# Two layers of a perceiver: VectorE's side work of a turn split in two parts, one ahead of each copy of transposed exponentials

## The chip, the cores and the metric

The kernel runs on one core of one Trainium2 chip. The metric is device time in microseconds (us) of one execution; the times given are medians of several runs. TensorE is called PE here, VectorE DVE, ScalarE ACT, GpSimd POOL and SyncE SP, as in the profile.

## The reference

The input x holds 64 sequences of 32 rows with 256 features, the context 64 sequences of 257 rows. Six blocks are added to x one after the other; each works on a layer norm of x:

```python
x = x + L0_xattn(layernorm(x), ctx, ctx)   # 16 heads of 16, rope, a window of 65 keys
x = x + L0_attn(layernorm(x))              # causal self-attention, rope
x = x + L0_ffn(layernorm(x))               # linear with fp8 rounding, below
x = x + L1_xattn(layernorm(x), ctx, ctx)   # softmax attention over all 257 keys
x = x + L1_mixer(layernorm(x))             # gated cumulative sum plus a convolution, below
x = x + L1_moe(layernorm(x))               # shared expert + top 2 of 8 experts, exact gelu

# L0_ffn, per row
scale = max(amax(abs(x)), 1e-12) / 448
A = (x / scale).astype(float8_e4m3fn).astype(f32) * scale
out = A @ (weight * weight_scale).T + bias

# L1_mixer
h = relu(x @ gate_w1 + gate_b1); gate = sigmoid(h @ gate_w2 + gate_b2)
glob = gate * (x @ U_w) * cumsum(x @ V_w, axis=1)
t_out = x[s-1] * conv_w[:, 0] + x[s] * conv_w[:, 1] + x[s+1] * conv_w[:, 2]
out = t_out + glob @ out_w + out_b
```

## The kernel before, in words

The 2048 rows of x lie in SBUF as 4 groups (g) of 4 tiles (t) of 128 rows, so 16 tiles; a tile is 4 sequences.

**Layer 0.** `small_attentions` (line 247) runs both small attentions as one pipeline of tiles; an iteration of its loop `for t` takes one tile through each of several stages. Behind the transposes of an iteration it calls a generator of side work twice (lines 588 and 589). For the last iterations that generator is `first_sides` (line 1431), which steps the fp8 linear of group 0.

**The fp8 linear** is the generator `linear(g)` (line 683), for one group of 512 rows: the norm; the row maxima `am` and from them the scales `xsc`, `rsc`, `osc` (three small VectorE instructions); the scaling of y by rsc (four GpSimd instructions); then, for each pair of tiles, `rounded(pair)` (line 709): two instructions that make `big` out of the exponent bits of y, and two sums that round, y + big and from that q = y - big. `by_feature` (line 723) transposes both q on PE (into ps_qT, copied by ScalarE), and `outputs` multiplies (ps_ff) and adds to x, scaled by osc. Each `yield` ends a step.

**Layer 1's cross-attention** (`cross_attention`, line 1018) is where most of the time lies: 16 tiles of 4 turns (b, one sequence each), 64 turns, numbered 0 to 63 here, and a tail. A turn mixes stages of two or three tiles. In its order in the loop (lines 1374 to 1405):

1. `turned(before, b, 0, eT)`: 4 PE transposes of the exponentials e of the tile before into ps_t, and a VectorE copy of that to eT.
2. `weights()`: the softmax sums of the turn before: VectorE's reciprocal, which waits for ScalarE's last exponential, then GpSimd's scaling of e (four instructions) by it.
3. `own_heads()` (every second turn): two VectorE instructions that take ps_o into own; the first waits for lv from GpSimd. In turn b = 1 `project` (ps_p, added to x by VectorE).
4. `values` (ps_v, 8 matmuls), copied by ScalarE.
5. `turned(before, b, 1, eT)`: the other 4 transposes. ps_t has a single bank, so they wait for the copy of step 1. Copied by VectorE, in the last tile by ScalarE.
6. `next(side, None)`: one step of side work.
7. `keys` of the next tile (ps_k), `scores` of this tile (ps_s, 16 matmuls into 4 banks; for each bank a VectorE reduction, which subtracts the mask and finds the row's extreme, and ScalarE's exponential), in turn b = 1 `last_keys` (ps_le, lv), `context` (ps_o, which reads eT and v).

All instructions of these stages keep their written order on each engine: a VectorE instruction that waits holds back everything written after it. So the order in the program is the order in each queue.

**The side work** of turn 16g and after is `side_work(g + 1)` (line 1326): linear(g + 1), then norm and queries of the next group. The row maxima with the scales come in turns 3, 19 and 35; `rounded(0)` in turns 5, 21, 37; `rounded(1)` in turns 6, 22, 38; `by_feature` of both pairs in turns 7, 23, 39. In the last 16 turns it is `late_pieces` (line 989): the mixers of groups 0, 1, 2 and the first half of 3, and the layer norms of the last block, each started at its own turn.

**The mixer** (`mixer`, line 764): norm; yT = transposed y (psT); ps_huv, scanned by VectorE; the gate (ps_g); for each of two channels c a matmul (ps_d) and three VectorE passes that make the convolution `conv` (taps 1, 0, 2; 128x512 elements, the first reads ps_d); then conv is transposed back (ps_x) and added to x. psT, ps_huv, ps_g, ps_d, ps_x, ps_qT, ps_ff, ps_k and ps_v share a ring of PSUM banks, so each also waits until an earlier tenant of its bank has been read. Channel 0's passes of mixers 0, 1, 2 lie in turns 55, 58, 61, channel 1's in 56, 59, 62, and ps_x in 57, 60, 63.

**The mixture** (`mixture`, line 1475) follows: router, top 2, experts. It also steps the mixer of the last two tiles (`last_mixer`).

Most instructions pass through one helper, so their line in the profile is 107 (all but PE), 119 (matmuls) or 122 (PE transposes); the names of the tiles tell them apart.

Of the kernel before, what the change touches and what calls it, by code (L numbers as in the profile page):

```python
# [11 lines left out]
AF = mybir.ActivationFunctionType  # L12
ALU = mybir.AluOpType
# [5 lines left out]
NB, S, SK = 64, 32, 257  # L19
H, DH = 16, 16  # L20
NG, NT = 4, 4
# [44 lines left out]
def perceiver_kernel(ctx: ExitStack, tc: tile.TileContext, a: dict, out: bass.AP):  # L66
# [613 lines left out]
        )  # L680
        yield

    def linear(g):

        x = xs[g]
        y = yield from norm_steps(g)

        for t in range(NT // 2):
            gpsimd.tensor_tensor(x[:, t], x[:, t], row(R_FF), ALU.add)
        yield  # L690
        am = small.tile([P, NT], F32, tag="am", name="am")
        vector.tensor_reduce(am, y, AX.X, ALU.max, apply_absolute_value=True)
        xsc = small.tile([P, NT], F32, tag="xsc", name="xsc")
        vector.tensor_scalar(xsc, am, 1e-12, 1.0 / 448.0, ALU.max, ALU.mult)
        rsc = small.tile([P, NT], F32, tag="rsc", name="rsc")
        vector.reciprocal(rsc, xsc)
        osc = small.tile([P, NT], F32, tag="osc", name="osc")
        vector.tensor_scalar(osc, xsc, vec[:, V_WS : V_WS + 1], None, ALU.mult)
        for t in range(NT // 2, NT):
            gpsimd.tensor_tensor(x[:, t], x[:, t], row(R_FF), ALU.add)  # L700
        yield
        for t in range(NT):
            gpsimd.tensor_scalar(
                y[:, t], y[:, t], rsc[:, t : t + 1], 1.0, ALU.mult, ALU.mult
            )
        yield
        qs, qTs = [], []

        def rounded(pair):


            v = y[:, 2 * pair : 2 * pair + 2, :]
            big = sb.tile([P, 2, D], F32, tag="big", name="big")
            vector.tensor_scalar(
                big.bitcast(I32), v.bitcast(I32), 0x7F800000, None, ALU.bitwise_and
            )
            vector.tensor_scalar(big, big, 2.0**-6, 1.5 * 2.0**20, ALU.max, ALU.mult)
            vector.tensor_tensor(v, v, big, ALU.add)
            q = sb.tile([P, 2, D], BF16, tag=f"fq{pair}", name="q")
            vector.tensor_tensor(q, v, big, ALU.subtract)  # L720
            qs.append(q)

        def by_feature(pair):
            ps = shared_bank[0]([P, 2, 2 * P], "ps_qT", BF16)
            for c in range(2):
                for i in range(2):
                    turn(ps[:, c, i * P : (i + 1) * P], qs[pair][:, i, c * P : (c + 1) * P], ident_bf)
            qT = sb.tile([P, 2, 2 * P], BF16, tag=f"fqT{pair}", name="qT8")
            scalar.copy(qT, ps)
            qTs.append(qT)  # L730

        def outputs(pair):
            ps = shared_bank[0]([P, 2, D], "ps_ff")
            for i in range(2):
                proj(
                    ps[:, i, :],
                    lambda k: qTs[pair][:, k, i * P : (i + 1) * P],
                    lambda k: w8[:, k, :],
                )
            for i in range(2):  # L740
                t = 2 * pair + i
                x = xs[g][:, t, :]
                vector.scalar_tensor_tensor(
                    x, ps[:, i, :], osc[:, t : t + 1], x, ALU.mult, ALU.add
                )

        rounded(0)
        yield
        rounded(1)
        yield  # L750
        by_feature(0)
        by_feature(1)
        yield
        outputs(0)
        yield
        outputs(1)
# [7 lines left out]
    def mixer(g, ts, eng=None, by_act=True):  # L764

        n, t0, N = len(ts), ts[0], len(ts) * P
        x = xs[g]
        steps = norm_steps(g, eng, True, ts, by_act)
        next(steps)
        yield  # L770
        next(steps)
        yield
        if n > 2:
            next(steps)
            yield
        y = finish(steps)

        for t in ts:
            gpsimd.tensor_tensor(x[:, t], x[:, t], row(R_GO), ALU.add)
        yield  # L780
        yT = transposed(y, shared_bank[0], mixer_yT([P, 2, N], "yT"))
        yield

        ps = shared_bank[0]([P, N], "ps_huv")
        proj(ps, lambda k: narrow[:, k, 0:P], lambda k: yT[:, k, :])
        hub = hubs([P, N], "hub")
        scalar.activation(hub[0:64], ps[0:64], AF.Relu, bias=vec[0:64, V_GB1 : V_GB1 + 1])
        sums = sb.tile([P, N], F32, tag="r2", name="sums")
        for i in range(n):
            at = slice(i * P, (i + 1) * P)  # L790
            vector.tensor_tensor_scan(
                sums[32:64, at], keep[96:P], ps[96:P, at], 0.0, ALU.mult, ALU.add
            )
        vector.scalar_tensor_tensor(hub[64:96], sums[32:64], 0.5, ps[64:96], ALU.mult, ALU.mult)
        yield

        ps = shared_bank[0]([P, N], "ps_g")
        mm(ps, lhsT=gw2, rhs=hub[0:64], start=True, stop=True)
        gate = sums[64:96]
        scalar.activation(gate, ps[64:96], AF.Tanh, bias=half_b[64:96], scale=0.5)  # L800
        vector.scalar_tensor_tensor(hub[64:96], gate, 1.0, hub[64:96], ALU.add, ALU.mult)
        yield
        conv = []
        for c in range(2):
            ps = shared_bank[0]([P, N], "ps_d")
            mm(ps, lhsT=gow[:, c * P : (c + 1) * P], rhs=hub[0:96], start=True, stop=True)

            def tap(i):
                return vec[:, V_CONV + 3 * c + i : V_CONV + 3 * c + i + 1]

            got = convs([P, N], "conv")
            src = yT[:, c, :].rearrange("p (b s) -> p b s", s=S)
            dst = got.rearrange("p (b s) -> p b s", s=S)
            vector.scalar_tensor_tensor(got, yT[:, c, :], tap(1), ps, ALU.mult, ALU.add)
            vector.scalar_tensor_tensor(
                dst[:, :, 1:S], src[:, :, 0 : S - 1], tap(0), dst[:, :, 1:S], ALU.mult, ALU.add
            )
            vector.scalar_tensor_tensor(
                dst[:, :, 0 : S - 1], src[:, :, 1:S], tap(2), dst[:, :, 0 : S - 1], ALU.mult, ALU.add
            )  # L820
            conv.append(got)
            if n > 2 or c == 1:
                yield
        for pair in range(n // 2):
            ps = shared_bank[0]([P, 2, D], "ps_x")
            for i in range(2):
                at = slice((2 * pair + i) * P, (2 * pair + i + 1) * P)
                for c in range(2):
                    turn(ps[:, i, c * P : (c + 1) * P], conv[c][:, at], ident)
            mine = x[:, t0 + 2 * pair : t0 + 2 * pair + 2, :]  # L830
            vector.tensor_tensor(mine, ps, mine, ALU.add)
# [157 lines left out]
    def late_pieces():  # L989
# [12 lines left out]
            (16, last_pieces[1]),  # L1002
        ]
        for now in range(20):
            for first, piece in pieces:
                if now >= first and (now, first) != (19, 14):
                    next(piece, None)
                    if now == first == 13:
                        next(piece)
                    if (now, first) == (18, 13):  # L1010
                        fill_hidden(1)
            fill_hidden({17: 1, 18: 2}.get(now, 0))
            yield
# [4 lines left out]
    def cross_attention(loaded):  # L1018
# [292 lines left out]
        now = fetched.pop(0)  # L1311
# [14 lines left out]
        def side_work(g):  # L1326
# [17 lines left out]
            yield  # L1344
            queries(yT, 1, qT_next[0])

        qT_next = [qT]
        last_sides = late_pieces()


        done, before = None, None
        weights, own_heads = None, None
        for i in range(nt + 2):
            g, t = divmod(i, NT)
            after = None
            if i < nt:
                if t == 0:
                    side = side_work(g + 1) if g + 1 < NG else last_sides
                now.update(g=g, t=t, e=[], qb=qb_next)
                now["last"] = last_([P, 4, 4], "last")  # L1360
                if i + 2 < nt:
# [12 lines left out]
            for b in range(4 if i <= nt else 0):  # L1374
# [7 lines left out]
                weights, own_heads = None, None  # L1382
                if done is not None and b == 1:
                    project(done)
                if before is not None:
                    v = values(before, b)
                    turned(before, b, 1, eT, i == nt - 1)
                    if b == 0:
                        spread(before)
# [40 lines left out]

    def first_sides():

        steps = linear(0)
        yield next(steps)
        yield
        yield next(steps)
        yield next(steps)
        yield next(steps)
        yield next(steps)
        yield  # L1440
        yield next(steps)
        yield
        yield next(steps)
        yield
        yield next(steps)
        yield next(steps)
        finish(steps)
# [27 lines left out]
    def mixture():  # L1475
# [25 lines left out]
        sync.dma_start(out=rc, in_=a["route"])  # L1501
        before_bf = sb.tile([P, 2, P], BF16, tag="fq0", name="before_bf")
        norm_1, norm_2, first_norm = last_pieces
        last_mixer = mixer(3, range(2, 4), vector, False)
        last_norm = normed(3, range(2, 4), vector, False)
        early, late = choose(0, nt - 4), choose(nt - 4, 4)
        warm = small.tile([P, 1], F32, tag="warm", name="warm")
# [537 lines left out]
```

## Time and profile before

| | us |
|---|---|
| median of 3 runs | 910.21 (908.77 to 911.31) |
| the profiled execution | 908.4 |
| its span, first to last instruction | 906.6 |
| PE busy in the span | 852.0 |
| DVE busy | 586.5 |
| POOL busy | 505.4 |
| ACT busy | 428.2 |
| mean granted PE clock | 0.983 |

By stretch, PE is busy for 255.9 of the first 280 us, 49.8 of the next 50, 128.7 of 130 (330 to 460), 127.5 of 130 (460 to 590), 83.0 of 90 (590 to 680), 52.8 of 60 (680 to 740) and 154.4 of the last 166.

A line of a timeline reads: start in us from the span's start, duration, engine, program line, operation, output tile <- input tiles, shapes and types, how many instructions are drawn together; in brackets the engine's idle time just before and the engine and tile whose semaphore ended it. The releaser is inferred; where the engine named had long been done, it was another.

### The profile page before, as it was taken

The page shows a single profiled execution, that of the slowest core. Times are in us where ns is not written, and L with a number is a line of the kernel's source. Part 1 is how long each engine was busy: PE and PEld are TensorE (multiplying, and loading weights), DVE is VectorE, ACT ScalarE, POOL GpSimd, SP SyncE. Part 2 cuts the span into 40 slices and gives each one's busy share as a digit, 9 for nine tenths or more (in the row PEclk, how much of TensorE's full clock was granted, in tenths as well). Part 3 has the DMA queues.
Part 4 walks back from the last instruction along what each step waited for, and adds up shares of the span by engine and source line. Part 5 has one row for each costly group of instructions (what it writes and reads, how often), then busy time and mean ns, then how long its engine had stood idle before and what let it go on. Part 6 is the DMA issues. An engine that isn't in the chain of part 4 may idle for free.

```text
span 906.6 us, 22805 instructions
## 1 busy us (share of the span) xinstructions
PE 852.0 (94%) x8699; PEld 586.0 (65%) x8699; DVE 586.5 (65%) x1717; ACT 428.2 (47%) x1107; POOL 505.4 (56%) x992
## 2 busy tenths in 40 slices
PE   6899999989899999999999999999898889999995
PEld 3466666665466666666666666565566558888884
DVE  6887777897677667675876666777765851111117
ACT  2566666654554555554554647555443322222220
POOL 3477777864765666564754748564652344555330
PEclk9999999989999999999999999999899999999998
DMA  7555434543111011111111113000001057777757
GB/s 239 145 138 142 91 92 104 132 118 106 54 54 38 18 53 55 53 55 53 48 26 35 54 54 100 2 1 2 25 24 36 24 169 212 232 232 232 225 172 270
DMA packets 66926, 88.77 MB, mean 98 GB/s; under 512 B 32480, under 2 KB 50688, under 8 KB 64768
## 3 DMA queue, kind: packets, MB, share of 16 engines
q1 hardware_dynamic: 63264, 77.73, 28.5%
q0 software_dynamic: 3456, 9.44, 3.1%
q8 instruction: 69, 1.13, 0.5%
q14 instruction: 41, 0.34, 0.1%
q10 hardware_dynamic: 96, 0.13, 0.1%
HBM read 65.78 MB, written 13.11 MB: 87 GB/s over the span
## 4 chain that ended last, share of the span: by engine, by line
PE 69%; DVE 18%; ACT 4%; POOL 3%; issue 3%; DMA 2%; SPq 0%; DVEq 0%; ACTq 0%; POOLq 0%
PE ps_v L119 12%; PE ps_o L119 11%; PE ps_k L119 10%; PE ps_h L119 7%; PE ps_t L122 7%; PE ps_qk L119 4%; PE ps_s L119 4%; PE ps_p L119 3%; DVE x L107 3%; ACT e L107 2%; DVE y L107 2%; PE ps_q L119 2%; PE pair_bank L119 1%; POOL sq L107 1%; PE psT L122 1%
## 5 line engine op out<-in xcount | busy, mean ns | idle before, releaser
L107 ACT ACTIVATE e<-e,xnm 128x257 f32<-128x257 f32 x256 | 127.2, 499 | 50.8 <-DVE xnm L107 45.3
L107 DVE CUSTOM_DVE_ANT_0 e<-ps_s,mask 128x257 f32<-128x257 f32 x256 | 93.4, 420 | 50.0 <-PE ps_s L119 49.6
L119 PE MATMUL ps_k<-ct,w_w_l1x 128*128 128x512 f32 x256 | 122.3, 600 | 1.6 <-ACT yT L107 0.6
L119 PE MATMUL ps_v<-w_w_l1x,ct 128*128 128x256 f32 x512 | 122.1, 382 | 0.0
L107 POOL TENSOR_SCALAR e<-e,xsm 128x256 f32<-128x256 f32 x256 | 121.2, 492 | 0.0
L122 PE MATMUL ps_t<-cst,e 128*128 128x128 f32 x640 | 102.8, 284 | 7.7 <-DVE eT L107 6.8
L107 DVE COPY eT<-ps_t 128x512 f32<-128x512 f32 x124 | 85.2, 687 | 28.7 <-PE ps_t L122 28.5
L119 PEld LDWEIGHTS ps_v<-w_w_l1x,ct 128*128 128x128 f32 x512 | 94.3, 192 | 11.1 <-issue 0.2
L107 ACT ACTIVATE kT<-ps_k,vec 128x512 f32<-128x512 f32 x64 | 44.0, 688 | 100.7 <-PE ps_k L119 100.4
L107 POOL TENSOR_TENSOR x<-x,rows 128x256 f32<-128x256 f32 x96 | 70.9, 753 | 36.1 <-ACT y L107 18.0
L122 PEld LDWEIGHTS ps_t<-cst,e 128*128 128x128 f32 x640 | 72.1, 142 | 26.3 <-DVE eT L107 7.6
L107 ACT ACTIVATE hTr<-ps_h,w 128x256 f32<-128x256 f32 (+1 forms) x80 | 31.4, 450 | 105.9 <-issue 82.7
L107 DVE TENSOR_TENSOR og<-ps_o,b 128x512 f32<-128x512 f32 (+1 forms) x20 | 12.8, 638 | 105.6 <-PE ps_o L119 105.6
L119 PEld LDWEIGHTS ps_k<-ct,w_w_l1x 128*128 128x128 f32 x256 | 44.5, 190 | 41.3 <-issue 35.3
L1811 POOL DMA_INDIRECT r_rows<-og,lv x36 | 35.5, 986 | 61.0 <-DVE og L107 56.1
L119 PE MATMUL ps_h<-ygT,w 128*128 128x256 f32 (+1 forms) x320 | 67.5, 365 | 0.1
L119 PE MATMUL ps_o<-w,hTr 128*128 128x256 f32 x288 | 65.3, 379 | 0.0
L107 ACT COPY v<-ps_v 128x512 f32<-128x512 f32 x80 | 46.4, 581 | 39.2 <-PE ps_v L119 39.0
L107 POOL TENSOR_TENSOR last<-e,xsm 128x4 f32<-128x4 f32 x64 | 12.9, 202 | 88.6 <-DVE xsm L107 88.6
L119 PEld LDWEIGHTS ps_h<-ygT,w 128*128 128x128 f32 x320 | 56.1, 194 | 6.7 <-issue 0.3
L119 PEld LDWEIGHTS ps_o<-w,hTr 128*128 128x128 f32 x288 | 54.4, 190 | 7.2
L107 ACT ACTIVATE kb<-kT,cst 128x256 f32<-128x256 f32 x96 | 45.3, 511 | 27.2 <-POOL kT L107 25.5
(208 smaller groups left out, 1658.1 us busy)
## 6 DMA issues: line engine op xcount, KB each, us to landing
ct<-in_ctxT SPq DMA_DIRECT2D x16, 1024.0 KB, 5.2
w<-in_ew SPq DMA_DIRECT2D x20, 514.0 KB, 4.0
w<-in_ew SPq DMA_DIRECT2D x20, 512.0 KB, 4.3
far<-part SPq DMA_DIRECT2D x126, 64.0 KB, 2.3
v_rows<-v SPq DMA_DIRECT2D x16, 256.0 KB, 2.3
vb<-v_rows SPq DMA_DIRECT2D x64, 64.0 KB, 2.2
r<-r_rows SPq DMA_DIRECT2D x8, 512.0 KB, 8.2
b<-in_eb SPq DMA_DIRECT2D x20, 128.0 KB, 3.9
```

The costliest lines, as they stand in the source:

```text
L107: ins = getattr(self.engine, name)(*args, **kw)
L119: return kept(nc.tensor.matmul(ps, **args))
L122: return kept(nc.tensor.transpose(ps, src, eye))
L1811: wrote = nc.gpsimd.indirect_dma_start(out=r_rows, out_offset=bass.IndirectOffsetOnAxis(ap=write_i[:, at : at + 1], axis=0), in_=o[:, i, : ...
```

## The change

VectorE's side work of a turn is put at two places of the turn. A list `pending` takes closures; `catch_up()` runs them, between step 3 and step 4 above, which in VectorE's queue is between the reciprocal (with own and the projection's add) and the second copy of eT. What is put on the list runs in the next turn there. Four things go on it: the three small scale instructions, the two rounding sums of a pair, and the third pass of each convolution channel. So the sums of pair 0 run in turns 6, 22, 38, those of pair 1 in turns 7, 23, 39; the third pass of channel 0 in turns 56, 59, 62, of channel 1 in turns 57, 60, 63.

The side generator is now stepped twice a turn. `in_halves` makes the first of the two an empty step for `side_work`; `late_pieces` does the same, except that the statistics of mixer 3's first half move to the first place of turn 61.

In group 0 (`first_sides`) the four scalings of y go from GpSimd to ScalarE, two of them one step later, and the scales' and sums' closures run at set steps. In the mixture the last mixer's third passes run after both channels' first two.

```diff
+    pending = []
+
+    def catch_up():
+        while pending:
+            pending.pop(0)()
+
+    def at_once(steps):
+        for _ in steps:
+            catch_up()
+            yield
+        catch_up()
+
-    def linear(g):
+    def linear(g, by_act=False):
...
-        vector.tensor_scalar(xsc, am, 1e-12, 1.0 / 448.0, ALU.max, ALU.mult)
-        vector.reciprocal(rsc, xsc)
-        vector.tensor_scalar(osc, xsc, vec[:, V_WS : V_WS + 1], None, ALU.mult)
+        def scales():
+            vector.tensor_scalar(xsc, am, 1e-12, 1.0 / 448.0, ALU.max, ALU.mult)
+            vector.reciprocal(rsc, xsc)
+            vector.tensor_scalar(osc, xsc, vec[:, V_WS : V_WS + 1], None, ALU.mult)
+
+        pending.append(scales)
...
-        for t in range(NT):
-            gpsimd.tensor_scalar(
-                y[:, t], y[:, t], rsc[:, t : t + 1], 1.0, ALU.mult, ALU.mult
-            )
+        def scaled(ts):
+            for t in ts:
+                if by_act:
+                    scalar.activation(y[:, t], y[:, t], AF.Copy, scale=rsc[:, t : t + 1])
+                else:
+                    gpsimd.tensor_scalar(
+                        y[:, t], y[:, t], rsc[:, t : t + 1], 1.0, ALU.mult, ALU.mult
+                    )
+
+        scaled(range(2 if by_act else NT))
         yield
...
             vector.tensor_scalar(big, big, 2.0**-6, 1.5 * 2.0**20, ALU.max, ALU.mult)
-            vector.tensor_tensor(v, v, big, ALU.add)
             q = sb.tile([P, 2, D], BF16, tag=f"fq{pair}", name="q")
-            vector.tensor_tensor(q, v, big, ALU.subtract)
             qs.append(q)
+
+            def sums():
+                vector.tensor_tensor(v, v, big, ALU.add)
+                vector.tensor_tensor(q, v, big, ALU.subtract)
+
+            pending.append(sums)
...
         rounded(0)
+        if by_act:
+            scaled(range(2, NT))
         yield
         rounded(1)
...
-            vector.scalar_tensor_tensor(
-                dst[:, :, 0 : S - 1], src[:, :, 1:S], tap(2), dst[:, :, 0 : S - 1], ALU.mult, ALU.add
+            pending.append(
+                lambda dst=dst, src=src, last=tap(2): vector.scalar_tensor_tensor(
+                    dst[:, :, 0 : S - 1], src[:, :, 1:S], last, dst[:, :, 0 : S - 1], ALU.mult, ALU.add
+                )
             )
...
         for now in range(20):
+            if now == 13:
+                next(pieces[4][1])
+            yield
             for first, piece in pieces:
                 if now >= first and (now, first) != (19, 14):
                     next(piece, None)
-                    if now == first == 13:
-                        next(piece)
...
+        def in_halves(steps):
+            for _ in range(4 * NT):
+                yield
+                next(steps, None)
+                yield
...
-                    side = side_work(g + 1) if g + 1 < NG else last_sides
+                    side = in_halves(side_work(g + 1)) if g + 1 < NG else last_sides
...
                 if done is not None and b == 1:
                     project(done)
+                catch_up()
+                next(side, None)
                 if before is not None:
                     v = values(before, b)
                     turned(before, b, 1, eT, i == nt - 1)
...
     def first_sides():
-        steps = linear(0)
+        steps = linear(0, True)
         yield next(steps)
         yield
         yield next(steps)
         yield next(steps)
         yield next(steps)
+        catch_up()
         yield next(steps)
         yield
         yield next(steps)
-        yield
+        yield catch_up()
         yield next(steps)
-        yield
+        yield catch_up()
         yield next(steps)
...
-        last_mixer = mixer(3, range(2, 4), vector, False)
+        catch_up()
+        last_mixer = at_once(mixer(3, range(2, 4), vector, False))
```

## The prediction, made before the changed kernel was run

> **What bounds the kernel now.** I read the busy table first: TensorE (PE) is busy for 94% of the span, VectorE (DVE) for 65%, GpSimd (POOL) for 56%.
>
> ```profile
> PE 852.0 (94%) x8699; PEld 586.0 (65%) x8699; DVE 586.5 (65%) x1717; ACT 428.2 (47%) x1107; POOL 505.4 (56%) x992
> ```
>
> Second, the busy time by stretch, which says where PE is not full. Columns: stretch, its length, then busy us of PE, PEld, DVE, ACT, POOL, granted clock, DMA share, GB/s.
>
> ```profile
> 330.00:460.00 130.00, 128.71 (x1438) 83.17 (x1437) 92.41 (x313) 70.32 (x211) 80.68 (x189) 1.00 0.15 47
> 590.00:680.00 90.00, 82.97 (x770) 54.20 (x769) 65.71 (x193) 46.83 (x119) 50.43 (x137) 0.94 0.04 13
> ```
>
> A whole group of 16 turns (330 to 460) leaves 1.3 us of PE idle, so the loop is bound by PE and a VectorE edit can win only what stands in such gaps. Third, PE's timeline at those gaps. Turn 22 to 23 (scores of turn 22 start at 364.83):
>
> ```profile
> 366.53 1.89 PE L119 MATMUL ps_v<-w_w_l1x,ct 128*128 128x256 f32 x8
> 369.25 0.66 PE L122 MATMUL ps_t<-cst,e 128*128 128x128 f32 x4 [0.84 <-DVE eT L107]
> 369.75 0.91 PE L122 MATMUL ps_qT<-ident_bf,q 128*128 128x128 bf16 x8
> ```
>
> The second four transposes (ps_t at 369.25) use the bank of the first four and wait for its copy eT. Fourth, VectorE's timeline shows why the copy is late:
>
> ```profile
> 363.24 0.68 DVE L107 COPY eT<-ps_t 128x512 f32<-128x512 f32 x1
> 363.84 0.43 DVE L107 TENSOR_SCALAR big<-y 128x512 int32<-128x512 int32 x1
> 364.31 0.59 DVE L107 TENSOR_SCALAR big<-big 128x512 f32<-128x512 f32 x1
> 364.93 0.84 DVE L107 TENSOR_TENSOR y<-y,big 128x512 f32<-128x512 f32 x1
> 365.80 1.42 DVE L107 TENSOR_TENSOR q<-y,big 128x512 bf16<-128x512 f32 x1
> ...
> 368.52 0.68 DVE L107 COPY eT<-ps_t 128x512 f32<-128x512 f32 x1
> 369.79 0.18 DVE L107 RECIPROCAL xsm<-xsm 128x4 f32<-128x4 f32 x1 [0.59 <-ACT e L107]
> ```
>
> The queue has no idle from 363.24 on: the rounding holds back the four score reductions (367.14), they the copy. The reciprocal follows the first reduction by 2.65. A stall-free plain turn takes 5.67 on PE.
>
> **The change, part by part.** The order of PE's and SyncE's instructions is untouched; VectorE's moves; GpSimd loses and ScalarE gains four scalings in the first group.
>
> *Rounding sums (groups 1 to 3; turns 6-7, 22-23, 38-39).* The two sums of pair 0 move from turn 21 into turn 22, ahead of the eT copy of 363.24; those of pair 1 leave turn 22 for turn 23, behind its reciprocal. Turn 22 so keeps two sums before its reductions; only their neighbours change. Beside GpSimd's scaling of e they cost .84 and .85 (rows at 253.36 and 254.24); alone .69 and .69 (358.53); beside the mask 1.42 (above). New queue from 363.24: sum .88, sum .77 (start to start), copy .60, big .47, big .62 = 3.34, reductions at 366.58 instead of 367.14: -.56. The two bigs now lie beside the mask instead, so I keep -.3: the gap of .84 shrinks, but stays. Turn 23: reciprocal at 369.49, +.10, sums .88 + .85, so q of pair 1 is there at 371.32. The same turn transposes both pairs: the second half of ps_qT was due at 369.75 + .46 = 370.21. It waits until 371.32: **+1.1** a group, with the earlier reductions already in it. Three groups +3.3; turn 5 is relieved of .13. **+3.2**. Ends: with every row as beside an idle GpSimd (357.57 to 359.87: big .50, .46, sums .73, .61, copy .60, sum 2.90) reductions at 366.14, reciprocal at 368.79 and q at 370.31, +.1 each, +.2 in all; with sums of 1.64 (row at 191.00) and 1.42 and nothing won before, +2.8 each, +8.4. I take the rows beside the scaling of e, since that starts right behind the same reciprocal.
>
> A rule speaks against this place. The Trainium skill, "SBUF — State Buffer", section "SBUF: two separate sides", says the port pair of VectorE and GpSimd is an exclusive lock: a VectorE instruction with two SBUF inputs and a GpSimd one reading SBUF shut each other out for a whole instruction. A scaling of e takes .48, so by the rule each sum could wait .48, 1.38 + .96 = 2.34 a pair, an estimate from that page, and this part would be about +5; the rows show only .15 a sum.
>
> *Scales.* In turn 3 the reductions start at 242.96, right behind osc; without the three small steps at 242.36: -.6 of the gap of 1.02 at 245.16. Turns 19 and 35 lose .09 each. They now run behind the next reciprocal, where eT waits for nothing in turn 4, and the scaling of y that needs them starts only at 250.72. **-.8** (ends -.9 and -.4).
>
> *Convolution, third pass (turns 55 to 63).* Nothing stalls before turn 57. Turn 57: the pass of channel 1 now stands behind the projection's add (600.40) and ends at 601.25; ps_x, which reads it, started at 600.53.
>
> ```profile
> 600.53 1.11 PE L122 MATMUL ps_x<-cst,conv 128*128 128x128 f32 x8
> 602.07 1.12 PE L119 MATMUL ps_g<-hub,gw 64*128 64x512 f32 x2 [0.43 <-DVE x L107]
> ```
>
> ps_x gets 601.25, its add then 601.9 to 602.6, ps_g 602.65: **+.6**. Turn 60:
>
> ```profile
> 626.40 0.63 PE L122 MATMUL ps_t<-cst,e 128*128 128x128 f32 x4 [0.91 <-POOL rn L107]
> 626.86 1.12 PE L122 MATMUL ps_x<-cst,conv 128*128 128x128 f32 x8
> 628.29 1.12 PE L119 MATMUL ps_g<-hub,gw 64*128 64x512 f32 x2 [0.30 <-DVE x L107]
> ```
>
> The gap of .91 (really the eT copy, 626.26) does not go: in turn 59 the scan behind the convolution waits for ScalarE's relu (ends 620.98) and starts at 621.01 however short the passes before it are. The pass of channel 1 comes after own (627.56) and takes .75, so ps_x starts at 628.35 instead of 626.86 and ps_g at 629.75: **+1.45**. Turns 61 to 63:
>
> ```profile
> 642.37 0.66 PE L122 MATMUL ps_t<-cst,e 128*128 128x128 f32 x4 [2.90 <-DVE eT L107]
> 645.81 1.11 PE L122 MATMUL psT<-cst,y 128*128 128x128 f32 x4 [0.31 <-DVE conv L107]
> ```
>
> Before the reductions .74 of statistics (moved into the 1.22 idle before 635.41) and one pass of 1.05 go: -1.7 at 642.37. It is given back: own waits for GpSimd's lv, which stands behind a chain that can start only at 639.58, when GpSimd's adds end (640.09 now), so own comes at 643.85 instead of 644.36; then channel 0's third pass (.75) stands before channel 1's first, and that ends at 646.05. The second psT waits for it: 646.1 for 645.81. **+.3**. In turn 66 channel 1's first pass comes .5 earlier and psT (gap .76 at 678.02) with it: **-.45**; the mixer in the mixture reads both channels after the same sum of passes: 0. Ends for these four: a pass of .73 and the clock kept full after 642 give +.5, passes of 1.08 give +3.
>
> *First group (184 to 202).* PE's rows:
>
> ```profile
> 191.02 1.13 PE L119 MATMUL ps_p<-w_w_l0a,cT 128*128 128x256 f32 x4 [1.90 <-ACT cT L107]
> 194.35 0.69 PE L122 MATMUL ps_c<-cst,o 128*128 128x128 f32 x2 [0.97 <-DVE o L107]
> ```
>
> cT waits in ScalarE's queue behind kb, that for GpSimd's kT, that behind the four scalings of y (1.85 at 185.56). On ScalarE they fit into its 1.65 idle before 186.28, so kT comes 1.75 earlier, and ps_c about 2. But VectorE has no gap from 184.84 to 201.9, and its work is the same: the sums only change places, pair 1's to the end, just ahead of the second ps_qT, at 201.95 instead of 201.3. **+.65**. Ends: the slow rows there (big 1.31, q 1.64, .83, .85) shrink to .47 to .69, -2.3, and PE's half clock goes with it: -3; the new idle before ps_qT brings a half-clock stretch, +3.
>
> **Sum:** +3.2 -.8 +.6 +1.45 +.3 -.45 +.65 = +4.95 on the profiled 908.4 (span 906.6 and 1.8 around it): 913.4. The median of the runs shown is 1.8 above the profiled one, so I forecast **915.2**.
>
> **Rivals.** *The half-clock stretches go; no change.* The granted clock is halved in two stretches behind the long gaps:
>
> ```profile
> 642.99:649.81 6.82, 6.51 (x63) 3.72 (x62) 5.34 (x14) 3.28 (x8) 4.56 (x12) 0.50 0.00 1
> 192.43:199.25 6.82, 5.85 (x89) 4.95 (x89) 6.65 (x15) 2.82 (x7) 5.21 (x6) 0.50 0.63 159
> ```
>
> If the smaller gaps (1.90 to under 1; 2.90 to 1.2) keep it full, the first is worth up to 5.85/2 = 2.9 plus the .65 above, the second 1.4 (scores, context and transposes of turn 62 at 1.09, 1.01, .89 for .62, .58, .49): 4.95 - 3.55 - 1.4 = 0, 910.2. For it: the gaps shrink. Against: VectorE is the limit in the first, and the second psT still waits, with PE idle for some 4 us before it.
>
> *VectorE and GpSimd stop hindering each other; faster.* If sums behind the reciprocal run at .69 and the slow rows of the first group go: rounding +.2, first group -3, scales -.8, convolution +2.35 - 1.4 (full clock in turn 62), turn 66 -.45, sum -3.1: 907.1. It holds from where a pair of sums takes under 1.45 there. Against it: .84 and .85 beside e.
>
> *New half-clock stretches; slower still.* Turn 60 has .48 + 1.49 idle on PE in one stretch of 3.41, turn 62 some 4, the first group 2.7. The gap of 1.90 at 191.02 came before a half-clock stretch. Each new one costs up to 3.41/2 = 1.7; three, +5: 920.3. The Trainium skill, "TensorE: Matmul & The Clock Gate", section "Why this matters for your kernels", sets the limit at idle gaps above about 3 us: by it only turn 62 is in danger, an estimate of +1.7. The trace halves after less.
>
> *It doesn't do what it says:* excluded, as each engine runs its instructions in the order written, and VectorE's order is a new one.
>
> **Chances.** Forecast .46, clock kept .24, faster .14, slower still .16. The range leaves out most of the faster case and the top of the slowest: 908 to 920. What can be told from no change is .3%, 2.7 us. A little of the forecast's own spread (its ends above) falls within .3%: faster .15, same .27, slower .58.
>
> **What would show it.** Right: a wait of ps_qT for VectorE's q of about 1.5 in turns 7, 23 and 39, with the gap before ps_t still there at about half; ps_x waiting for conv in turns 57 (.7) and 60 (1.5); the gap at 642.37 down to about 1.2, and a longer one before the second psT; turn 3 shorter by .6. Wrong: sums of .69 beside e, or the reductions in turn 22 a full microsecond earlier; then ps_qT waits for nothing and the gaps are gained.

## The result and the profile after

The changed kernel takes 913.08 us (median of 18 runs, 908.03 to 918.98) beside 910.0 (18 runs, 908.07 to 912.68): ratio 1.0028, 95% interval 1.0016 to 1.0041, so 1.5 to 3.7 us slower. The forecast was 915.2, the range 908 to 920: the right side and inside the range, but the loss is about half of the 4.95 worked out. The profiled execution took 912.1, its span 910.3.

Its busy table (columns as before):

```profile
PE 854.0 (94%) x8699; PEld 587.4 (65%) x8699; DVE 585.4 (64%) x1717; ACT 431.0 (47%) x1111; POOL 506.1 (56%) x988
```

ACT has four instructions more and POOL four fewer, DVE the same number: work was moved, none removed. PE's waits from 229 us to 680 us (who waited for whom: us in total, times, longest):

```profile
PE ps_qT L122 <- DVE q L107: 3.6, 3, 1.2
PE psT L122 <- DVE conv L107: 3.5, 5, 2.0
PE ps_t L122 <- DVE eT L107: 2.6, 3, 2.1
...
PE ps_x L122 <- DVE conv L107: 1.2, 1, 1.2
```

Before, the wait of ps_t for eT was 6.8 in six places and that of psT for conv 2.4; ps_qT and ps_x did not wait at all. 4.2 us of the old wait went, and 3.6 + 1.2 + 1.1 of new waits came. The places shown next are those of the prediction; turn 22 starts .54 us later here than before. PE, turns 22 and 23:

```profile
369.10 0.66 PE L122 MATMUL ps_t<-cst,e 128*128 128x128 f32 x4
369.59 0.39 PE L122 MATMUL ps_qT<-ident_bf,q 128*128 128x128 bf16 x4
371.19 0.40 PE L122 MATMUL ps_qT<-ident_bf,q 128*128 128x128 bf16 x4 [1.21 <-DVE q L107]
371.42 1.94 PE L119 MATMUL ps_k<-ct,w_w_l1x 128*128 128x512 f32 x4
```

The gap ahead of ps_t is nearly gone, and ps_qT falls into two parts with a gap of 1.21 between. VectorE in the same turns:

```profile
359.81 0.43 DVE L107 CUSTOM_DVE_ANT_0 e<-ps_s,mask 128x257 f32<-128x257 f32 x1 [0.77 <-PE ps_s L119]
...
362.48 0.18 DVE L107 RECIPROCAL xsm<-xsm 128x4 f32<-128x4 f32 x1 [0.19 <-ACT e L107]
...
363.19 0.73 DVE L107 TENSOR_TENSOR y<-y,big 128x512 f32<-128x512 f32 x1
363.95 0.85 DVE L107 TENSOR_TENSOR q<-y,big 128x512 bf16<-128x512 f32 x1
364.73 0.68 DVE L107 COPY eT<-ps_t 128x512 f32<-128x512 f32 x1
365.33 0.56 DVE L107 TENSOR_SCALAR big<-y 128x512 int32<-128x512 int32 x1
365.92 1.15 DVE L107 TENSOR_SCALAR big<-big 128x512 f32<-128x512 f32 x1
366.99 0.41 DVE L107 CUSTOM_DVE_ANT_0 e<-ps_s,mask 128x257 f32<-128x257 f32 x1
...
369.63 0.18 DVE L107 RECIPROCAL xsm<-xsm 128x4 f32<-128x4 f32 x1 [0.59 <-ACT e L107]
369.73 0.66 DVE L107 TENSOR_TENSOR y<-y,big 128x512 f32<-128x512 f32 x1
370.42 0.71 DVE L107 TENSOR_TENSOR q<-y,big 128x512 bf16<-128x512 f32 x1
```

CUSTOM_DVE_ANT_0 is the score reduction; the first of a turn's four is shown. q of pair 1 is made only after the reciprocal, for which VectorE stood idle .59. Turn 60 on PE, and the two waits of turn 61:

```profile
627.10 0.63 PE L122 MATMUL ps_t<-cst,e 128*128 128x128 f32 x4 [0.91 <-POOL rn L107]
627.57 0.27 PE L122 MATMUL ps_x<-cst,conv 128*128 128x128 f32 x1
629.04 0.99 PE L122 MATMUL ps_x<-cst,conv 128*128 128x128 f32 x7 [1.20 <-DVE conv L107]
...
643.80 0.66 PE L122 MATMUL ps_t<-cst,e 128*128 128x128 f32 x4 [2.06 <-DVE eT L107]
...
648.05 1.12 PE L122 MATMUL psT<-cst,y 128*128 128x128 f32 x4 [2.00 <-DVE conv L107]
```

In turn 60 the old gap of .91 stays, and ps_x stops after its first transpose, which needs only channel 0.

Where the time went is read from the rows of scores in both traces: row n lasts on PE from the first score matmul of turn n to that of turn n + 1, so it holds the second transposes and the side work of turn n + 1. The differences, in us: row 3 -.69, row 4 +.67, 5 -.19, 6 -.18, 19 and 35 -.08 each, 22 and 38 +.03 each, 56 +.17, 59 +1.38, 60 +.19, 61 and 62 together +.02; every other is within .02. That is +1.3 from scores 0 to scores 63. The second psT of turn 66 gives -.52. The first scores come at 230.13 for 229.12, although this execution was .51 ahead at 150.8, where nothing is changed: +1.5 for the first group. Together +2.3, within the interval of the timed runs. Behind 700 us this profile loses 1.7 more (with eight ps_sh matmuls at half clock, 6.14 for 3.68). The last mixer's convolution just ahead has its passes in a new order, but that does not decide it: two later profiles with these passes in place lose 1.8 in the same part (698.9 to 740 us of the profile before), and two with them moved lose nothing.

### The profile page after: what moved, and what is told of

Same layout as the page of the kernel before. It is cut to its first block, busy times and chain, and to the rows that moved or that the text cites. A ratio compares the mean times of both kernels' runs of the same rounds, so it can differ in the third digit from the quotient of the medians.

```text
span 910.3 us, 22808 instructions
## 1 busy us (share of the span) xinstructions
PE 854.0 (94%) x8699; PEld 587.4 (65%) x8699; DVE 585.4 (64%) x1717; ACT 431.0 (47%) x1111; POOL 506.1 (56%) x988
## 4 chain that ended last, share of the span: by engine, by line
PE 67%; DVE 17%; POOL 5%; ACT 5%; issue 3%; DMA 2%; SPq 0%; ACTq 0%; DVEq 0%; POOLq 0%
PE ps_v L119 11%; PE ps_o L119 11%; PE ps_k L119 10%; PE ps_h L119 7%; PE ps_t L122 7%; PE ps_qk L119 4%; PE ps_s L119 4%; PE ps_p L119 3%; DVE x L107 3%; ACT e L107 2%; PE ps_q L119 2%; PE ps_sh L119 1%; DVE y L107 1%; PE pair_bank L119 1%; POOL sq L107 1%
## 5 line engine op out<-in xcount | busy, mean ns | idle before, releaser
L107 POOL TENSOR_SCALAR e<-e,xsm 128x256 f32<-128x256 f32 x256 | 124.1, 503 | 0.0
L107 POOL TENSOR_TENSOR last<-e,xsm 128x4 f32<-128x4 f32 x64 | 14.8, 231 | 89.5 <-DVE xsm L107 89.5
```

The lines of the kernel that those rows point to most:

```text
L107: ins = getattr(self.engine, name)(*args, **kw)
```

## The experiments

Theory after the result: the loss is the sum of those local parts, and the large one is order: a piece put behind the reciprocal waits for ScalarE's last exponential, and what needs the piece in the same turn waits with it. Rivals: the moved sums cost 3 us, as forecast; or the loss is in half-clock stretches, not in the order.

Three runs undo one part each, a fourth puts the transposes of q a turn later; all were timed beside the same runs of the kernel before (909.87).

**The sums of groups 1 to 3 back in place.**

```diff
-            pending.append(sums)
+            if by_act:
+                pending.append(sums)
+            else:
+                sums()
```

> The changed kernel with the two rounding sums of groups 1 to 3 back in their old place; all else as changed. Theory of the parts (read from the two traces): the moved sums win .7 to .9 us ahead of the second transposes and lose .8 at ps_qT, so undoing them is worth 0 to +.3 us: the turns from scores 22 and 38 take 7.89 again instead of 7.92, and the median stays within 1 us of the changed kernel (912.5 to 914 beside 910.0 of the kernel before). Rival, the forecast's term: the moved sums cost 3.2 us, so undoing them gives the kernel before, 910, or less.

Measured: 911.79, ratio 1.0021 (1.0006 to 1.0035); rows 22 and 38 take 7.90 for 7.92, rows 5 and 6 .39 more together. The move of the sums was worth nothing either way; the forecast's 3.2 us are not there. The median is 1.3 under the changed kernel's, a little below the band expected; the two intervals overlap.

This run shows something else: its rows 59 and 60, the same code as in the changed kernel, took 17.21 for 14.96; 1.49 of that comes back in row 61, where PE waits for VectorE, so that rows 59 to 62 lose 1.0 in all. The granted clock of that stretch (columns: stretch, length, busy us of PE, PEld, DVE, ACT, POOL, clock, DMA share, GB/s):

```profile
628.90:635.73 6.83, 6.83 (x62) 3.94 (x61) 4.09 (x12) 3.46 (x10) 3.35 (x8) 0.50 0.01 2
```

It follows the same gaps of .91 and 1.20 that the changed kernel's own profile passed at full clock. Five profiles of these runs have both gaps: two show this stretch behind them (the other one with the transposes of q a turn later, 17.11 in rows 59 and 60), three do not. None of the seven profiles without the gap of 1.20 shows it.

**The third convolution passes back in place.**

```diff
-            pending.append(
-                lambda dst=dst, src=src, last=tap(2): vector.scalar_tensor_tensor(
-                    dst[:, :, 0 : S - 1], src[:, :, 1:S], last, dst[:, :, 0 : S - 1], ALU.mult, ALU.add
-                )
-            )
+            vector.scalar_tensor_tensor(
+                dst[:, :, 0 : S - 1], src[:, :, 1:S], tap(2), dst[:, :, 0 : S - 1], ALU.mult, ALU.add
+            )
```

> The changed kernel with the third convolution passes back in place; the early statistics of mixer 3 stay early. Theory of the parts: ps_x no longer waits in turns 57 and 60, so the rows of scores 56, 59 and 60 lose .17, 1.38 and .19, and turn 66 gains its .5 back as a loss: -1.3 in all, about 911.7. In turn 61 the gap before the second ps_t is about 2.2, from 2.9 before, since only the statistics have left the queue. Rival, the clock: the added time of the changed kernel comes from half-clock stretches that fall anywhere, then the median does not move, 913, with a mean clock of .979 again.

Measured: 909.65, ratio .9999 (.9983 to 1.0015). Rows 56, 59 and 60 take 9.26, 7.44 and 5.99, as before the change. The convolution's move is a loss. Row 61 takes 10.93 for 11.56 before the change, but the early statistics account for .17 of that, ahead of the second psT. The other .46 is the clock: PE takes .59 from the second psT to the next scores at full clock here, 1.05 at half clock in the profiles of both kernels. The gap before the second ps_t is 2.71, not the expected 2.2: the four small VectorE steps behind the statistics (mv, ve, half, r) took 1.48, beside GpSimd's adds, for 1.03 before. By the rows scores 0 to 63 take 2.4 less than in the changed kernel, .46 of it clock, and turn 66 gives .52 back, so 1.4; 1.3 was expected. The drop of the ratio is 2.9 thousandths, 2.6 us; the intervals leave room for 1.4, and stretches like the one above may make up the rest, which is not shown.

**The first group as before.**

```diff
-        steps = linear(0, True)
+        steps = linear(0)
...
-        catch_up()
...
-        yield catch_up()
+        yield
-        pending.append(scales)
+        if g:
+            pending.append(scales)
+        else:
+            scales()
-            pending.append(sums)
+            if g:
+                pending.append(sums)
+            else:
+                sums()
```

> The changed kernel with the first group's linear as before (y scaled by GpSimd, scales and sums at once). Theory of the parts: the wait of 2.16 of ps_qT for q at 200.9 and the two half-clock stretches after it go, the gaps of 1.90 and .97 at ps_p and ps_c come back; net -1.6 us at the first scores of layer 1, about 911.5. Rival: the earlier start of the first group is a gain that only shows later, then this is slower than the changed kernel, 914 to 915.

Measured: 909.74, ratio 1.0000 (.9984 to 1.0017), 2.5 us under the changed kernel. The half-clock stretches did not go: this profile has 10.24 us of them from 191.39. One profile cannot price this part of the kernel: with the first group's code of before, the first scores came 0, .5, 1.2 and .4 us late in four profiles (counted from 150.8), with the changed code 1.5, .2, 1.6, 1.7, 2.8 and 1.5 in six. The means differ by 1.0.

**The transposes of q a turn later.**

```diff
         rounded(1)
         yield
+        if g:
+            yield
         by_feature(0)
...
             yield from linear(g)
-            yield
             y = yield from norm_steps(g)
```

> The changed kernel with both transposes of q one turn later (turns 8, 24, 40) in groups 1 to 3, and the empty step behind the linear left out, so that no other step but the outputs moves. Theory of the parts: the wait of 1.21 of ps_qT goes and the gain ahead of the second transposes stays, -.77 in each of three groups, -2.3 in all: 910.7; the rows of scores 22 and 38 together with the next lose .75. Rival: VectorE's queue is what ends last either way, then the wait comes back at another tile of the next turn and the median stays at 913.

Measured: 911.29, ratio 1.0001 (.9984 to 1.0018). The wait at ps_qT is gone, and rows 6 to 10 of a group take .53 less in all (.77 expected; a gap of .15 ahead of ps_t and waits for ScalarE's copy of q remain). So the sums' move does have a gain, which the wait of ps_qT had eaten. The median is .6 above the expected one, and the interval overlaps with the changed kernel's.

The next four were run beside 909.86.

**GpSimd's bias adds a turn later**, for the gain of row 3 that row 4 gave back:

```diff
-        for t in range(NT // 2, NT):
-            gpsimd.tensor_tensor(x[:, t], x[:, t], row(R_FF), ALU.add)
+        def last_adds():
+            for t in range(NT // 2, NT):
+                gpsimd.tensor_tensor(x[:, t], x[:, t], row(R_FF), ALU.add)
+
+        if not g:
+            last_adds()
         yield
...
         scaled(range(2 if by_act else NT))
+        if g:
+            last_adds()
         yield
```

> The changed kernel with GpSimd's two later bias adds of the linear (1.41 us) one turn later, behind qb. In the trace of the changed kernel the .69 won by the scales in turn 3 comes back in turn 4, where the second half of the scores waits .24 for qb, which stands behind those adds in GpSimd's queue. If that is the cause, the row of scores 4 falls from 6.55 to 5.9 and the scores start in one piece; rows 3 and 19 stay at 5.61 and 5.67. Rival: turn 4 waits for something that the scales delay themselves (the copy of eT behind them); then the row stays at 6.55.

Measured in one execution: row 4 takes 5.67, as a plain turn does, and less than the 5.88 before the change. Its scores in the changed kernel, then in this one:

```profile
247.76 0.66 PE L119 MATMUL ps_s<-kT,qb 32*64 32x257 f32 x8
248.66 0.66 PE L119 MATMUL ps_s<-kT,qb 32*64 32x257 f32 x8 [0.24 <-POOL qb L107]
```

```profile
250.92 0.69 PE L119 MATMUL ps_s<-kT,qb 32*64 32x257 f32 x16
```

The scores split where they wait for qb, and run in one piece with the adds behind it. So qb was the cause. The single time, 914.92, says nothing here (a half-clock stretch in row 0 alone cost 1.4).

**The pieces ahead of the reciprocal.** One call moves:

```diff
+                catch_up()
                 if weights:
                     weights()
...
-                catch_up()
                 next(side, None)
```

> The changed kernel with the moved pieces ahead of the reciprocal instead of behind it. VectorE is idle for .59 there, and q of pair 1 no longer depends on ScalarE's last exponential: the wait of 1.21 at ps_qT falls to about .6, and ps_x in turn 60 comes some .7 earlier; -.6 in three groups, -.7, together about -2.5 against the changed kernel, 910.6. Rival: the reciprocal, own and GpSimd's scaling behind it are late instead; then the next turn's scores or context wait as long, and the median stays at 913 or more.

Measured: 905.42, ratio .9943 (.9927 to .9958): 4.4 us under the kernel before by the medians (5.2 by the ratio) and 7.7 under the changed one, from nothing but the order of the reciprocal and the moved pieces; three times what was expected. Rows 6, 22 and 38 take 6.84 for 7.92, rows 59 to 62 32.17 for 35.45 (.46 of that is the end of row 61 at full clock again). Scores 0 to 63 together take 421.2, for 427.9 in the changed kernel and 426.6 before: the gain stands where the pieces moved. VectorE in turns 22 and 23:

```profile
362.23 0.69 DVE L107 COPY eT<-ps_t 128x512 f32<-128x512 f32 x1
362.84 0.68 DVE L107 TENSOR_TENSOR y<-y,big 128x512 f32<-128x512 f32 x1
363.55 0.69 DVE L107 TENSOR_TENSOR q<-y,big 128x512 bf16<-128x512 f32 x1
364.16 0.17 DVE L107 RECIPROCAL xsm<-xsm 128x4 f32<-128x4 f32 x1
...
368.09 0.69 DVE L107 COPY eT<-ps_t 128x512 f32<-128x512 f32 x1
368.69 0.68 DVE L107 TENSOR_TENSOR y<-y,big 128x512 f32<-128x512 f32 x1
369.41 0.69 DVE L107 TENSOR_TENSOR q<-y,big 128x512 bf16<-128x512 f32 x1
```

and PE behind them:

```profile
369.43 0.60 PE L122 MATMUL ps_t<-cst,e 128*128 128x128 f32 x4
369.87 0.84 PE L122 MATMUL ps_qT<-ident_bf,q 128*128 128x128 bf16 x8
```

The sums stand where VectorE had waited for the last exponential, GpSimd is idle meanwhile, so each takes .68 or .69, and the reciprocal no longer waits. ps_t has no gap and ps_qT runs in one piece. I had expected about half of the wait at ps_qT to stay, and had not counted the .30 that was left ahead of ps_t; of rows 59 to 62 I had counted only .7 at ps_x.

**What was left over of the change, and the first group's two edits apart.** Both kernels leave the convolution in place, put the adds behind qb and the transposes of q a turn later; the pieces still stand behind the reciprocal. They differ in the first group:

```diff
-        steps = linear(0)
+        steps = linear(0, True)
```

The first has y scaled by GpSimd, the second by ScalarE, both with scales and sums at once.

> What the first runs leave over of the change: scales and rounding sums of groups 1 to 3 in the middle of the turn, with the transposes of q a turn later and the bias adds a turn later; the early statistics; the first group and the convolutions as before. By the local rows: scales -.7, three groups of -.5, turn 61 -.6 and the first group 0, together -2.8: 907 beside 910. Rival, the clock: the local gains are eaten by half-clock stretches elsewhere, 909 to 911.

> As the one before, with the first group's y scaled by ScalarE but its sums at once, in VectorE's old order. It tells the two edits of the first group apart. If the late sums made the loss there (the wait of 2.16 at ps_qT), this one starts the scores of layer 1 some .5 to 2 us earlier than the one before, since kT no longer waits behind the scalings: 905 to 906.5. If the scalings on ScalarE made it, it is slower than the one before by about 1.5.

Measured: 906.28, ratio .9953 (.9934 to .9971), and 905.52, .9948 (.9933 to .9964). The intervals do not tell the two apart; the first scores do: -1.05 with ScalarE, counted as above, for 0 to 1.2, and -1.05 again in the last run below. So it was the late sums, or the scales that were late with them, that lost in the first group, not the scaling on ScalarE; the wait of 2.16 for q points to the sums. Of the .6 counted for turn 61, .13 to .15 is order in these two profiles; the rest is clock, as above.

The last two were run beside 909.21. **The sums and scales alone ahead of the reciprocal**, with the convolution and the first group as before (the diffs above together):

> The changed kernel with the first group and the convolution as before, and the scales and rounding sums of groups 1 to 3 ahead of the reciprocal. By the place theory (a piece behind the reciprocal waits for ScalarE's last exponential, a piece ahead of it fills VectorE's idle .6) three groups win 1.05 each against the kernel before, the scales nothing net, the early statistics .6: about -3.9, 906. Rival: the gain of the run with all pieces early came from the convolution or the first group; then this one is at 909 to 910.

Measured: 905.06, ratio .9959 (.9946 to .9971), 3.7 less. Rows 6, 22, 38 take 6.84 again: the gain of the place holds without the other parts. Rows 59 to 62 take 33.07, so the convolution's passes ahead of the reciprocal win another .9 against passes in place.

**All together:** pieces ahead of the reciprocal, adds behind qb, the first group by ScalarE with its sums at once.

> What the runs point to, together: the moved pieces ahead of the reciprocal, the two later bias adds of the linear behind qb, the first group's scaling on ScalarE with its sums at once. From the run with the pieces ahead of the reciprocal alone (905.4 beside 909.9): turn 4 saves .87, the first group 1 to 2, so 902 to 904. If the first group's gain was only where the half-clock stretches fell, 904.5 to 905.5.

Measured: 901.40, ratio .9918 (.9897 to .9940): 7.5 us under the kernel before by the ratio, the fastest of all and a little below the band expected. Row 4 takes 5.67, the first scores come 1.06 earlier than before, and scores 0 to 63 take 420.3 for 426.6: together 7.4 in this profile (.46 of it clock in row 61), so the local parts add up to about what was measured.

## Why the prediction was right and wrong

**Direction and waits: right.** All three new waits were forecast at their places: ps_qT for q (1.21 measured; about 1.5 forecast), ps_x for conv in turn 60 (row 59 +1.38; +1.45), the second psT for conv (the wait grew by 1.7 while ps_t's shrank by .84, rows 61 and 62 together +.02; +.3). The gap ahead of that ps_t was forecast to fall by 1.7, not .84; the four small steps behind the statistics took 1.97 beside GpSimd's adds for 1.03 before. Turn 66 gave -.52 (-.45). That the total came inside the range is partly luck: the range is 12 us wide, and the rounding term, 3.5 too dear, was partly made up by the scales and the first group, about 1 too cheap together.

**The rounding sums: the step that failed.** Forecast +3.2 in three groups, measured -.3. In turn 22, counted from the same start (times of after less .54), three errors add up. Before the change the first reductions of turns 21 and 22 and the reciprocal of turn 22 stood here:

```profile
359.87 0.42 DVE L107 CUSTOM_DVE_ANT_0 e<-ps_s,mask 128x257 f32<-128x257 f32 x1
...
362.52 0.18 DVE L107 RECIPROCAL xsm<-xsm 128x4 f32<-128x4 f32 x1 [0.26 <-ACT e L107]
...
367.14 0.41 DVE L107 CUSTOM_DVE_ANT_0 e<-ps_s,mask 128x257 f32<-128x257 f32 x1
```

First, I began VectorE's queue at 363.24 as before, since PE does not stall in turn 21. But the sums that left turn 21 had held its reductions back by .60 (359.87; 359.27 now), and the reciprocal follows the reductions, so turn 22's queue begins .59 earlier (363.19 less .54 for 363.24). A queue's delay need not show on PE to be handed to the next turn. The second big took 1.15 beside the mask instead of .59, which took some of that back: the reductions came .69 earlier, not .30. Second, I priced sum pairs at 1.65 and 1.73 by the row beside GpSimd's scaling of e. They took 1.54 and 1.40: VectorE was hindered little, and GpSimd's scaling paid, which nobody waited for: 2.70 and 2.34 in these two turns, for 1.84 beside no sum.

```profile
362.90 2.70 POOL L107 TENSOR_SCALAR e<-e,xsm 128x256 f32<-128x256 f32 x4
...
370.42 2.34 POOL L107 TENSOR_SCALAR e<-e,xsm 128x256 f32<-128x256 f32 x4
```

Both together bring q .73 earlier than forecast. Third, I let the whole tail of ps_qT come after the wait; but the second four need only .23 to ps_k, and ScalarE's copy of the first half is done by then, so another .3 went. That makes 1.0 a group, nearly the whole term. The sign named for the gap ahead of ps_t, still there at about half, did not come either: it nearly went. The Trainium skill, "SBUF — State Buffer", section "SBUF: two separate sides", has the lock fall to whichever of the two starts first, the other being shut out; the estimate of +5 drawn from it was far off here: a sum beside the scaling took at most .85 for .69, and GpSimd lost most.

**The scales: the cover was there, but another wait behind it.** -.8 forecast, -.18 measured. Row 3 won .69 as worked out; row 4 gave .67 back, waiting for qb. I had checked the copy of eT in turn 4, not what GpSimd owed there; its queue keeps its own time when PE comes earlier.

**Turn 57:** +.6 forecast, +.17 measured. I let all of ps_x wait for channel 1; its first transpose needs channel 0 only, and the pass came sooner than assumed.

**The first group:** +.65 forecast, about +1.0 measured over several profiles. ps_qT waits there for the late sums, as forecast:

```profile
200.88 0.40 PE L122 MATMUL ps_qT<-ident_bf,q 128*128 128x128 bf16 x4 [2.16 <-DVE q L107]
```

The half-clock stretch behind the new idle, which the forecast's upper end of +3 counted on, came in the changed kernel's profile, though not at that price: the ps_c that stood at 200.82 before came 2.83 earlier, and the one after it, behind ps_qT and at half clock, 1.08 later than before.

**The rivals.** The half-clock stretches did not go with the smaller gaps: 6.82 us at 194.76 and 201.59, for 6.83 at 192.43 before. So the first rival did not come, and its 1.4 for turn 62 adds up to 1.3. The rival of new ones came true in some executions: such a stretch cost rows 59 to 62 1.0 in two of five profiles with the same gaps there. That sums and GpSimd stop hindering each other was half true: 1.40 is under its bound of 1.45, and its price for the sums, +.2, was near the -.3 measured, but the first group's -3 and the full clock in turn 62 did not come.

What stays open is how much of the 913.08 is clock: the 18 executions have mean clocks of .975 to .986, and the longest have the lowest; what decides whether a gap is followed by such a stretch is not settled.

## What to carry to other kernels

In an engine that keeps its program order, look for the instruction that waits for another engine (here the reciprocal, .59 idle) and put movable work ahead of it, not behind: the same pieces at the earlier call turned a loss of 3 us into a gain of 4.4. Before deferring a producer, find its consumer's due time in the same turn; and follow a removed delay through the engine's own queue into the next turn even where the bottleneck shows no gap, and into the other engines' queues that will be late next.

## What was not expected of the hardware

Between a VectorE sum with two inputs in SBUF and GpSimd's scaling most of the loss fell on GpSimd: .66 to .85 for a sum that takes .69 alone, 2.34 to 2.70 for four scalings that take 1.84 alone. A one-input instruction beside GpSimd's mask was hit harder: 1.15, for .59 beside the scaling and .43 alone.

The granted clock halved for 6.83 us behind PE gaps of .91 and 1.20 in two profiles and stayed full behind the same gaps in three others. The Trainium skill, "TensorE: Matmul & The Clock Gate", section "Why this matters for your kernels", warns of gaps above about 3 us; here such stretches followed shorter ones, though not always.
